# Layer 2 of a four-layer image network: from a scheduler's order to an order written out, with outer products moved to GpSimd

## The chip, the cores and the metric

The kernel runs on one core of one Trainium2 chip. A core has five engines that work side by side and wait for each other through semaphores: TensorE (PE in the profile, with its weight loads as PEld), VectorE (DVE), ScalarE (ACT), GpSimd (POOL) and SyncE (SP), which here only starts transfers. SBUF is the memory on the chip that they compute from, PSUM the one that TensorE writes to. The metric is the device time of one launch in microseconds. Before the change it is 10302.39 us, the median of three runs (10298.44 to 10305.17).

## What is computed

Four images of 256 channels and 64x64 pixels pass through four layers, each of the form `x = x + layer(group_norm(x))`: a deformable convolution (layer 0), an attention (layer 1), a deformable aggregation with 16 groups (layer 2) and a state-space scan (layer 3). The change touches layer 2 alone:

```
xp   = w_value . x + b_value                        # 256 channels = 16 groups x 16
om   = w_om . x + b_om                              # 432 = 16 groups x (9 points x (dx, dy) + 9 masks)
for each pixel (h, w), group g, point k of a 3x3 grid:
    sy, sx = h + ky[k] + dy[g,k],  w + kx[k] + dx[g,k]
    val    = bilinear sample of the zero-padded xp, group g, at (sy, sx)
    out[h, w, g, :] += mask[g,k] * val
y = w_out . out + b_out
```

Where no offset exceeds 1, every sample lies in a window of 5x5 pixels around its own. The kernel uses that: it works out, for each pixel and group, 25 shares (one for each place of the window) and sums 25 shifted copies of `xp` with them. If any offset does exceed 1, a last branch of the program computes everything anew in a slower way (`layer2_any`).

## The kernel before

The four images go one after the other; in each, layers 0 to 3 follow each other, and each needs the whole result of the one ahead. Layer 2 takes the image as 32 tiles. A tile is one row of the upper half of the image together with the row 32 below it, 2 x 64 = 128 pixels, one for each partition. The main loop (`for j0`) takes two tiles at a time (`T = 2`), so an image has 16 pairs.

For a pair the work is:

- `values(q)`: two rows of `xp` by matmuls (L701, L703), a copy into a ring of four tiles by ScalarE (L704), and eight transfers by SyncE (L708) that put the copies shifted by -2, -1, 1 and 2 pixels beside it. This is done for rows ahead of the pair.
- `shares(j0)`: offsets and masks by matmuls into a PSUM tile `pom` (L720, L723). ScalarE makes three weights of each offset, `relu(-o)`, `1 - |o|` and `relu(o)`, in `hat` (L727 to L730). VectorE takes the largest `|o|` for the test at the end (L732), multiplies one side's weights with the mask (L736, `mh`), forms the 3x3 outer products of the two sides (L744, `pr`, one instruction for each of two tiles), and adds them into the 5x5 shares `A` in PSUM, one instruction for each of 9 points and 2 tiles (L753). `A` has been cleared by ScalarE (L715). `shares` is a Python generator: the loop draws the next pair's steps between the products of the current pair.
- The five steps of the window (`for wy`): in each, VectorE multiplies five shifted copies with their shares, once for each of two tiles (L802, `prod`, three buffers); GpSimd adds the five products partly, four to two (L810); TensorE sums the remaining three into one PSUM tile `pd` by multiplying with the identity (L812).
- `finish`: ScalarE copies `pd` to SBUF (L820), TensorE transposes it (L762), ScalarE copies it back (L764), TensorE multiplies with `w_out` (L771), and VectorE adds the result to the image `x` (L780), with statistics for layer 3 at every fourth pair (L152). It is called during the next pair.

Within layer 2 the order of the code isn't the order on the engines: a scheduler places each engine's instructions, and the loop's order is its input. An engine runs its own instructions strictly in the order that they were placed in. `values`, `pt3` and `pz2` share one PSUM bank (`self.psum`), `pom` is one tile of two banks, and `A` has two tiles of two banks each.

Of the kernel before, what the change touches and what calls it, by code (L numbers as in the profile page):

```python
# [16 lines left out]
P = 128  # L17
# [46 lines left out]
class Net:  # L64
# [588 lines left out]
    def layer2(self, x):  # L653


        nc, tc = self.nc, self.tc
        gk, T = GRP * K2, 2
        with (
# [51 lines left out]
            def shares(j0):  # L710

                A = pshare.tile([P, T, 512], F32, tag="A", name="A")
                A = A[:, :, : GRP * WIN * WIN]
                made[j0] = A
                nc.scalar.copy(A, zero.rearrange("p (t u) -> p t u", u=1).to_broadcast([P, T, GRP * WIN * WIN]))  # L715
                A = A.rearrange("p t (g y x) -> p t g y x", y=WIN, x=WIN)
                po = pom.tile([P, T, 512], F32, tag="pom", name="pom")
                for t in range(T):
                    for ct in range(2):
                        nc.tensor.matmul(  # L720
                            po[:, t, : 3 * gk], xr[:, ct, j0 + t + 2, :], wom[:, ct, :], start=(ct == 0), stop=False
                        )
                    nc.tensor.matmul(po[:, t, : 3 * gk], self.halves[:, 0, :], bom, start=False, stop=True)  # L723

                hat = pb.tile([P, T, 2 * gk, 3], F32, tag="hat", name="hat")
                ab = pb.tile([P, T, 2 * gk], F32, tag="ab", name="ab")
                nc.scalar.activation(hat[:, :, :, 0], po[:, :, : 2 * gk], AF.Relu, scale=-1.0)  # L727
                nc.scalar.activation(hat[:, :, :, 2], po[:, :, : 2 * gk], AF.Relu)
                nc.scalar.activation(ab, po[:, :, : 2 * gk], AF.Abs)
                nc.scalar.activation(hat[:, :, :, 1], ab, AF.Identity, bias=1.0, scale=-1.0)  # L730
                yield
                nc.vector.tensor_reduce(  # L732
                    seen[:, j0 // T : j0 // T + 1], ab.rearrange("p t k -> p (t k)"), AX.X, ALU.max
                )
                mh = pb.tile([P, T, gk, 3], F32, tag="mh", name="mh")
                nc.vector.tensor_mul(  # L736
                    mh,
                    hat[:, :, 0:gk, :],
                    po[:, :, 2 * gk : 3 * gk].rearrange("p t (k u) -> p t k u", u=1).to_broadcast([P, T, gk, 3]),
                )  # L740
                yield
                pr = pb.tile([P, T, gk, 3, 3], F32, tag="pr", name="pr", bufs=1)
                for t in range(T):
                    nc.vector.tensor_mul(  # L744
                        pr[:, t],
                        mh[:, t].rearrange("p k (y x) -> p k y x", x=1).to_broadcast([P, gk, 3, 3]),
                        hat[:, t, gk : 2 * gk, :].rearrange("p k (y x) -> p k y x", y=1).to_broadcast([P, gk, 3, 3]),
                    )
                    yield
                for t in range(T):  # L750
                    for k in range(K2):
                        a = A[:, t, :, k // 3 : k // 3 + 3, k % 3 : k % 3 + 3]
                        nc.vector.tensor_add(a, a, pr[:, t, bass.ts(k, GRP), :, :])  # L753
                        if k % 3 == 2:
                            yield

            def finish(j0, o):
                oT = pb.tile([P, 2, 2, T, W], F32, tag="oT", name="oT")
                pt = self.ps("pt3")
                for ct in range(2):  # L760
                    for t in range(T):
                        nc.tensor.transpose(pt[:, bass.ts(2 * ct + t, P)], o[:, t, bass.ts(ct, P)], self.ident)  # L762
                for ct in range(2):
                    nc.scalar.copy(  # L764
                        oT[:, ct].rearrange("p h t x -> p t h x"),
                        pt[:, bass.ts(ct, T * P)].rearrange("p (t h x) -> p t h x", t=T, h=2),
                    )
                pz = self.ps("pz2").rearrange("p (o y) -> p o y", o=2)
                for ot in range(2):
                    for ct in range(2):  # L770
# [3 lines left out]
                            oT[:, ct].rearrange("p h t x -> p (h t x)"),  # L774
                            start=(ct == 0),
                            stop=(ct == 1),
                        )
                for ot in range(2):
                    xs = x[:, ot, :].rearrange("p (h y) -> p h y", h=2)[:, :, j0 * W : (j0 + T) * W]
                    nc.vector.scalar_tensor_tensor(  # L780
                        xs, pz[:, ot, :].rearrange("p (h y) -> p h y", h=2), bo[:, ot : ot + 1], xs, ALU.add, ALU.add
                    )
                    if j0 % 8 == 8 - T:
                        for h in range(2):
                            self.note(x, ot, 4 * h + j0 // 8)

            made, late = {}, None
            for q in range(3):
                values(q)
            for _ in shares(0):  # L790
                pass
            for j0 in range(0, HH, T):
                if j0 // VR + 3 < (HH + 4) // VR:
                    values(j0 // VR + 3)
                ahead = shares(j0 + T) if j0 + T < HH else iter(())
                A = made.pop(j0).rearrange("p t (g y x) -> p t g y x", y=WIN, x=WIN)
                pd = pacc.tile([P, T * 256], F32, tag="pacc", name="pacc")
                for wy in range(WIN):
                    prod = pb.tile([P, WIN, T, 256], F32, tag="prod", name="prod", bufs=3)
                    for t in range(T):  # L800
                        y = j0 + t + wy
                        nc.vector.tensor_mul(  # L802
                            prod[:, :, t, :].rearrange("p x (g c) -> p x g c", c=GC),
                            ring[y // VR % 4][:, :, y % VR, :].rearrange("p x (g c) -> p x g c", c=GC),
                            A[:, t, :, wy, :].rearrange("p g (x u) -> p x g u", u=1).to_broadcast([P, WIN, GRP, GC]),
                        )
                        next(ahead, None)
                    prod = prod.rearrange("p x t c -> p x (t c)")
                    for i in (0, 2):
                        nc.gpsimd.tensor_add(prod[:, i, :], prod[:, i, :], prod[:, i + 1, :])  # L810
                    for wx in (4, 0, 2):
                        nc.tensor.matmul(  # L812
                            pd, self.ident, prod[:, wx, :], start=(wy == 0 and wx == 4), stop=(wy == WIN - 1 and wx == 2)
                        )
                    if wy == 1 and late:
                        finish(*late)
                for _ in ahead:
                    pass
# [714 lines left out]
```

## Time and profile before

The profiled execution took 10256.01 us, and its span is 10254.2 us. In the first image layer 0 lies at about 0 to 620, layer 1 at 620 to 1138, layer 2 at 1138 to 1576 and layer 3 at 1576 to 2600.

| | PE | PEld | DVE | ACT | POOL | clock |
|---|---|---|---|---|---|---|
| whole span, share busy | 86% | 41% | 77% | 47% | 64% | 0.957 |
| layer 2, 1141.5 to 1575.9 (434.4 us), busy us | 387.41 | 165.89 | 408.59 | 94.61 | 242.24 | 0.98 |
| the same in image 2 (434.8 us) | 386.78 | 165.91 | 408.39 | 94.63 | 242.01 | 0.98 |
| image 3 (433.8 us) | 387.02 | 165.82 | 408.38 | 94.63 | 241.70 | 0.98 |
| image 4 (436.3 us) | 386.88 | 165.98 | 408.74 | 94.68 | 242.17 | 0.98 |

A row of the profile names the line of the kernel, the engine, the operation, the tile written and the tiles read (`prod<-ring,A`), the shape, and how often it ran. After the bar come busy time and the mean of one in ns, and after a second bar the time that the engine sat idle just before, with what ended that wait. "Clock" is the share of full speed that TensorE was granted. A timeline row has start and duration, and merges runs of like instructions (`x11`); an instruction's duration overlaps the next one's start, so what one costs in a row is read from start to start.

### The profile page before, as it was taken

Reading aid. Unit: us, or ns where it says so; the run is one execution under the profiler, and the core shown is the slowest. Engines: PE = TensorE matmul, PEld = TensorE weight load, DVE = VectorE, ACT = ScalarE, POOL = GpSimd, SP = SyncE. Lnnn points to the kernel's source line nnn. Section 1 sums busy time; section 2 is a strip of 40 time slices with the busy share of each in tenths; the row PEclk is TensorE's granted clock in tenths of the full one; section 3 lists DMA queues with packets and bytes.
Section 4 is the critical chain, followed back from the end, with each engine's and each line's share of the span. In section 5 each row is a group of like instructions: output and inputs, shape, how many; then the busy total and the mean of one; then the engine's idle time right before and its main releaser. Section 6 shows DMA issues by size and latency. Waiting matters only on the chain. (4 is left out here: it accounts for less than half of the span.)

```text
span 10254.2 us, 89063 instructions
## 1 busy us (share of the span) xinstructions
PE 8808.1 (86%) x29193; PEld 4231.4 (41%) x29193; DVE 7924.0 (77%) x8975; ACT 4869.3 (47%) x7460; POOL 6576.2 (64%) x3768
## 2 busy tenths in 40 slices
PE   5889998888788999889878898988977899888997
PEld 3643333333464333333346433333335643333333
DVE  4864697999675469799968546989996854798998
ACT  3743224665473322566557332256655733216664
POOL 3746556787474655688757465568875736556886
PEclk8999999999899999999989999999998999999999
DMA  7930111111782011111179101111118910111111
GB/s 264 328 109 1 37 40 35 44 45 49 269 315 97 1 37 40 36 45 46 45 286 325 70 1 41 36 40 48 44 43 321 322 36 1 45 41 37 40 41 34
DMA packets 377894, 956.57 MB, mean 93 GB/s; under 512 B 34676, under 2 KB 107821, under 8 KB 375373
## 3 DMA queue, kind: packets, MB, share of 16 engines
q0 software_dynamic: 165888, 604.05, 16.4%
q1 hardware_dynamic: 211532, 346.73, 10.6%
q8 instruction: 234, 3.83, 0.2%
q14 instruction: 240, 1.96, 0.1%
HBM read 784.59 MB, written 92.32 MB: 86 GB/s over the span
## 5 line engine op out<-in xcount | busy, mean ns | idle before, releaser
L1378 DVE TENSOR_TENSOR_SCAN h<-da,carry,h 128x512 f32<-128x512 f32 x2048 | 2470.6, 1264 | 140.2 <-ACT da L1377 91.4
L1392 POOL TENSOR_TENSOR h<-h,cn 128x2048 f32<-128x2048 f32 x508 | 2300.2, 4528 | 41.3 <-POOL carry L1389 0.6
L1377 ACT ACTIVATE da<-delta,l3a 128x512 f32<-128x512 f32 x2048 | 1388.7, 689 | 1145.5 <-DVE h L1378 1143.7
L1290 PE MATMUL y<-h,ident 128*128 128x512 f32 x4096 | 1920.9, 613 | 1.9 <-POOL h L1395 0.9
L344 POOL DMA_INDIRECT g<-tab,idx x1152 | 1343.7, 1166 | 761.0 <-issue 349.8
L548 POOL TENSOR_TENSOR acc<-acc,e 128x1024 f32<-128x1024 f32 x480 | 1125.3, 2344 | 541.0 <-ACT e L544 519.8
L810 POOL TENSOR_TENSOR prod<-prod 128x512 f32<-128x512 f32 x640 | 945.9, 1499 | 745.9 <-DVE prod L802 716.7
L388 PE MATMUL pz<-cols,l0w 128*128 128x256 f32 x4608 | 1213.6, 410 | 173.6 <-DVE cols L377 80.2
L1290 PEld LDWEIGHTS y<-h,ident 128*128 128x128 f32 x4096 | 806.0, 197 | 1289.3 <-issue 1236.8
L1370 DVE TENSOR_TENSOR h<-du,bn 128x2048 f32<-128x2048 f32 x512 | 1157.9, 2261 | 26.6 <-PE bn L1298 26.2
L465 DVE TENSOR_REDUCE m<-pm 128x3 f32<-128x1536 f32 (+1 forms) x372 | 602.3, 1625 | 716.8 <-PE pm L455 715.1
L353 DVE SCALAR_TENSOR_TENSOR r<-g,wx,r 128x512 f32<-128x512 f32 x1152 | 857.7, 745 | 352.3 <-ACT r L352 262.4
L812 PE MATMUL pacc<-prod,ident 128*128 128x512 f32 x1920 | 960.7, 623 | 142.7 <-POOL prod L810 106.2
L388 PEld LDWEIGHTS pz<-cols,l0w 128*128 128x128 f32 x4608 | 895.2, 205 | 341.5 <-DVE cols L377 117.7
L555 PE MATMUL cx<-e,v 128*128 128x512 f32 x2048 | 1001.4, 616 | 0.0
L544 ACT ACTIVATE e<-sc 128x1024 f32<-128x1024 f32 x512 | 496.0, 1020 | 1032.8 <-PE sc L531 1032.8
L802 DVE TENSOR_TENSOR prod<-ring,A 128x1280 f32<-128x1280 f32 x640 | 932.7, 1477 | 19.7 <-DMA ring<-ring 13.1
L352 ACT ACTIVATE r<-g,wx 128x512 f32<-128x512 f32 x1152 | 826.3, 717 | 254.8 <-DMA g<-tab,idx 209.2
L370 PE MATMUL pt<-ident,acc 128*128 128x128 f32 x2304 | 428.3, 293 | 302.0 <-DVE acc L361 197.5
L1389 POOL COPY carry<-h 128x4 f32<-128x4 f32 x512 | 98.3, 192 | 807.0 <-DVE h L1378 795.0
L812 PEld LDWEIGHTS pacc<-prod,ident 128*128 128x128 f32 x1920 | 325.9, 190 | 702.1 <-POOL prod L810 459.7
L555 PEld LDWEIGHTS cx<-e,v 128*128 128x128 f32 x2048 | 352.2, 189 | 598.9 <-issue 596.3
(247 smaller groups left out, 11219.4 us busy)
## 6 DMA issues: line engine op xcount, KB each, us to landing
cn<-cd SPq DMA_DIRECT2D x512, 256.0 KB
tab<-vt SPq DMA_DIRECT2D x112, 640.0 KB
ring<-ring SPq DMA_DIRECT2D x288, 126.0 KB
ring<-ring SPq DMA_DIRECT2D x288, 124.0 KB
g<-tab,idx POOLq DMA_INDIRECT x1152
x<-in_x SPq DMA_DIRECT2D x64, 256.0 KB
out<-x SPq DMA_DIRECT2D x56, 256.0 KB
l0w<-in_l0w SPq DMA_DIRECT2D x4, 2304.0 KB
```

Source lines behind the costliest of these rows:

```text
L344: nc.gpsimd.indirect_dma_start(out=g[:], out_offset=None, in_=tab[:, :], in_offset=bass.IndirectOffsetOnAxis(ap=idx[:, t, k : k + 1], axis=0),
L388: nc.tensor.matmul(sums[m][:, ot, :256], wf[:, i, bass.ts(ot, P)], cols[m][:, i, :], start=(i == 0), stop=(i == 17),)
L548: nc.gpsimd.tensor_add(b["acc"], b["acc"], e)
L555: nc.tensor.matmul(blocks[qb]["cx"], v[:, 4 * (i + kt // 4 * 4) + kt % 4, :], e[:, bass.ts(i % 2, 512)], start=(kt == 0 and i == 0), stop= ...
L802: nc.vector.tensor_mul(prod[:, :, t, :].rearrange("p x (g c) -> p x g c", c=GC), ring[y // VR % 4][:, :, y % VR, :].rearrange("p x (g c) - ...
L810: nc.gpsimd.tensor_add(prod[:, i, :], prod[:, i, :], prod[:, i + 1, :])
L812: nc.tensor.matmul(pd, self.ident, prod[:, wx, :], start=(wy == 0 and wx == 4), stop=(wy == WIN - 1 and wx == 2))
L1290: nc.tensor.matmul(c["ys"][dc], self.ident, h[:, dc, :], start=False, stop=(n == DS - 1))
L1370: nc.vector.tensor_mul(h, c["du"], c.pop(("bn", n)).to_broadcast([P, 4, C]))
L1377: nc.scalar.activation(da, c["delta"][:, dc, :], AF.Exp, scale=al[:, dc, n : n + 1])
L1378: nc.vector.tensor_tensor_scan(h[:, dc, :], da, h[:, dc, :], carry[:, dc, n : n + 1], ALU.mult, ALU.add)
L1392: nc.gpsimd.tensor_mul(h, h, cn.to_broadcast([P, 4, C]))
```

## The change

Layer 2's loop is written out for four engines (`tc.manual_schedule` for PE, Activation, DVE and Pool), so that each of them runs the instructions in the order of the code. SyncE's transfers are still placed by the scheduler. The generator is replaced by small functions, called from the five steps of each pair:

- `offsets(p + 2, t)` in steps 0 and 1, `hats(p + 2, ...)` in steps 2 and 3: a pair's offsets and weights are begun two pairs ahead. `values(p + 3)` stands in step 2.
- `masked(p + 1)` stands between the two products of step 0, `outer(p + 1, i)` in steps 0 to 2, `gather(p + 1, i)` in steps 2 to 4.
- `hat`, `mh` and `pr` hold the two tiles innermost by point, and `A` is one tile of 1024 elements in which groups and tiles lie together. One gather therefore serves both tiles: 9 instructions of 288 elements in place of 18 of 144.
- The outer products are three instructions of 864 elements on GpSimd. For the first pair two of the three stay on VectorE.
- `total`, the sum on TensorE, is called one step later than the additions whose results it reads. `turned` and `project` (parts of `finish`) come in steps 3 and 4 of the next pair, `finish` in step 1 of the one after.
- VectorE's maximum of `|o|` is replaced by a ScalarE instruction that sums `relu(|o| - 1)` as it goes, and the test at the end asks for more than 0 in place of more than 1.
- Ahead of the loop the first pair's offsets, hats and clearing come before the first `values`.

```diff
-                nc.vector.tensor_reduce(
-                    seen[:, j0 // T : j0 // T + 1], ab.rearrange("p t k -> p (t k)"), AX.X, ALU.max
-                )
...
-                for t in range(T):
-                    nc.vector.tensor_mul(
-                        pr[:, t],
-                        mh[:, t].rearrange("p k (y x) -> p k y x", x=1).to_broadcast([P, gk, 3, 3]),
-                        hat[:, t, gk : 2 * gk, :].rearrange("p k (y x) -> p k y x", y=1).to_broadcast([P, gk, 3, 3]),
-                    )
...
-                        nc.vector.tensor_add(a, a, pr[:, t, bass.ts(k, GRP), :, :])
...
+                    nc.scalar.activation(side(1), d["ab"], AF.Identity, bias=1.0, scale=-1.0)
+
+                    nc.scalar.activation(d["ab"], d["ab"], AF.Relu, bias=-1.0, accum_out=seen[:, p : p + 1])
...
+                engine.tensor_mul(
+                    d["pr"][:, bass.ts(i, n)],
+                    mh[:, bass.ts(i, n), :].rearrange("p k (y x) -> p k y x", x=1).to_broadcast([P, n, 3, 3]),
+                    hat[:, bass.ds(gk * T + i * n, n), :]
+                    .rearrange("p k (y x) -> p k y x", y=1)
+                    .to_broadcast([P, n, 3, 3]),
                 )
...
+                for k in range(3 * i, 3 * i + 3):
+                    a = A[:, :, i : i + 3, k % 3 : k % 3 + 3]
+                    nc.vector.tensor_add(a, a, made[p]["pr"][:, bass.ts(k, GRP * T)])
...
+                for t in range(T):
+                    offsets(0, t)
+                hats(0, 0)
+                hats(0, 1)
+                clear(0)
+                values(0)
+                masked(0)
+                for i in range(3):
+                    outer(0, i, nc.gpsimd if i == 1 else nc.vector)
+                values(1)
+                values(2)
+                for t in range(T):
+                    offsets(1, t)
+                for i in (0, 2, 1):
+                    gather(0, i)
+                hats(1, 0)
+                hats(1, 1)
+
+
+                behind = None
+                for p in range(last + 1):
+                    near, far = p < last, p < last - 1
+                    for wy in range(WIN):
+                        product(p, wy, 0)
+                        if near and wy == 0:
+                            masked(p + 1)
+                        product(p, wy, 1)
+                        if wy == 1 and p > 1:
+                            finish(p - 2)
+                        if near and wy > 1:
+                            gather(p + 1, wy - 2)
+                        if near and wy < 3:
+                            outer(p + 1, wy, nc.gpsimd)
+                        prod = pairs(p)
+                        if behind:
+                            total(*behind)
+                        behind = p, wy, prod
+                        if wy == 0:
+                            if near:
+                                clear(p + 1)
+                            if p:
+                                nc.scalar.copy(made[p - 1]["o"].rearrange("p t c -> p (t c)"), made[p - 1]["pd"])
+                        if far and wy < 2:
+                            offsets(p + 2, wy)
+                        if wy == 2:
+                            if far:
+                                hats(p + 2, 0)
+                            if p < last:
+                                values(p + 3)
+                        if wy == 3:
+                            if far:
+                                hats(p + 2, 1)
+                            if p:
+                                turned(p - 1)
+                        if wy == 4 and p:
+                            project(p - 1)
+                total(*behind)
...
-        nc.vector.tensor_scalar(i, m, 1.0, None, ALU.is_gt)
+        nc.vector.tensor_scalar(i, m, 0.0, None, ALU.is_gt)
```

## The prediction

> **What bounds the kernel now.** I first looked at which engine has no idle time in layer 2. A pair of tiles (a pass of the `j0` loop) takes 24.64 us: its first product starts at 1226.05 and the next pair's at 1250.69. The busy time of each engine in exactly that stretch (PE, PEld, DVE, ACT, POOL, then clock, DMA share, GB/s):
>
> ```profile
> 1226.05:1250.69 24.64, 22.95 (x62) 10.18 (x62) 24.20 (x34) 5.88 (x9) 14.93 (x10) 1.00 0.14 42
> ```
>
> VectorE is busy 24.20 of 24.64; TensorE looks almost as full, but its ends are modelled, so I go by starts. The groups of layer 2 from the list by shape say what the work is:
>
> ```profile
> L810 POOL TENSOR_TENSOR prod<-prod 128x512 f32<-128x512 f32 x640 | 945.9, 1499 | 745.9 <-DVE prod L802 716.7 <-PE pacc L812 28.3 <-DVE A L753 1.0
> L802 DVE TENSOR_TENSOR prod<-ring,A 128x1280 f32<-128x1280 f32 x640 | 932.7, 1477 | 19.7 <-DMA ring<-ring 13.1 <-DVE A L753 0.5
> ...
> L753 DVE TENSOR_TENSOR A<-A,pr 128x144 f32<-128x144 f32 x1152 | 358.2, 311 | 22.5
> ...
> L744 DVE TENSOR_TENSOR pr<-mh,hat 128x1296 f32<-128x1296 f32 x128 | 191.7, 1500 | 0.1
> ...
> L736 DVE TENSOR_TENSOR mh<-hat,pom 128x864 f32<-128x864 f32 x64 | 66.6, 1041 | 1.1 <-ACT hat L730 1.0
> ```
>
> L802 idles 19.7 us in 640 runs, and those mostly for ring copies: VectorE is the bound, and GpSimd waits for it (716.7). Durations overlap, so costs come from start to start in the timeline of VectorE (start, duration, count of the run):
>
> ```profile
> 1236.88 1.47 DVE L802 TENSOR_TENSOR prod<-ring,A 128x1280 f32<-128x1280 f32 x1
> 1238.28 0.30 DVE L753 TENSOR_TENSOR A<-A,pr 128x144 f32<-128x144 f32 x1
> 1238.49 1.47 DVE L802 TENSOR_TENSOR prod<-ring,A 128x1280 f32<-128x1280 f32 x1
> ...
> 1245.82 1.04 DVE L736 TENSOR_TENSOR mh<-hat,pom 128x864 f32<-128x864 f32 x1
> 1246.78 3.81 DVE L753 TENSOR_TENSOR A<-A,pr 128x144 f32<-128x144 f32 x11
> 1250.69 4.28 DVE L802 TENSOR_TENSOR prod<-ring,A 128x1280 f32<-128x1280 f32 x3
> ```
>
> A product costs 1.40; a gather between products 0.21; eleven in a row take 3.91, so one behind its forerunner costs 0.37 (it reads what that wrote). L736 costs 0.96; from the same timeline L744 1.41, L732 0.66, the two L780 0.785. Sum: 10 x 1.40 + 7 x 0.21 + 3.91 + 2 x 1.41 + 0.66 + 0.96 + 0.785 = 24.6, the period. Every fourth pair adds four statistics, 2.38.
>
> **VectorE after.** The outer products leave (2.82) and so does the maximum (0.66). The 18 gathers of 144 elements become 9 of 288. Elements cost (1.41 - 0.96) / (1296 - 864) = 1.04 ns, so 144 more cost 0.15: one alone 0.36, one behind its forerunner 0.52; three in a row 1.40, and three such groups 4.2 (before 5.4). No row shows the new layout of A (groups and tiles together), so I bound a group by 1.2 (forerunners cost nothing extra: 3 x 0.36, rounded up) and 2.0 (each as dear again as its elements), and take 1.40. New sum: 14.0 + 4.2 + 0.96 + 0.785 = 19.95, and with a quarter of 2.38, 20.5.
>
> **TensorE after.** Nothing is removed, only put in order. Start to start:
>
> ```profile
> 1228.26 1.72 PE L720 MATMUL pom<-l,xr 128*128 128x432 f32 x4
> 1229.91 0.35 PE L723 MATMUL pom<-bom,halvesb 3*128 3x432 bf16 x1
> 1230.19 1.98 PE L812 MATMUL pacc<-prod,ident 128*128 128x512 f32 x4
> ...
> 1237.94 1.03 PE L701 MATMUL pc<-l,xr 128*128 128x256 f32 x4
> ...
> 1240.38 8.25 PE L812 MATMUL pacc<-prod,ident 128*128 128x512 f32 x18
> ```
>
> Offsets of a tile: 1.93, twice 3.86. Values: 1240.38 - 1237.94 = 2.44. An L812 costs 0.43 (weight loads start 0.43 apart), 30 make 12.9. Four transposes 0.49, the projection 1.93. Sum 21.62. This exceeds VectorE's 20.5, so TensorE becomes the bound. The totals lie one step behind the products and offsets two pairs ahead, so TensorE should rarely wait; a hand-over from GpSimd costs 0.05 (end 1232.89, start 1232.94), and five a pair make 0.25. The granted clock is 1.00 here and where TensorE is fuller (720 to 1120, layer 1), so density costs no clock.
>
> **GpSimd after, and two rules.** It keeps ten additions and gets three products of 864 elements; no row shows a GpSimd operand with rows of three elements and a repeated one.
>
> ```profile
> 1229.08 3.81 POOL L810 TENSOR_TENSOR prod<-prod 128x512 f32<-128x512 f32 x2 [6.28 <-DVE prod L802]
> 1233.29 3.63 POOL L810 TENSOR_TENSOR prod<-prod 128x512 f32<-128x512 f32 x2 [0.40 <-DVE prod L802]
> 1238.50 2.50 POOL L810 TENSOR_TENSOR prod<-prod 128x512 f32<-128x512 f32 x2 [1.58 <-DVE prod L802]
> ```
>
> Two additions take 2.50 except beside L744, where they take 3.81 and 3.63. L548 does 1024 elements in 2.344 and L810 512 in 1.271 (its median), so an element costs (2.344 - 1.271) / 512 = 2.1 ns and an instruction 0.2 besides; 864 take 0.2 + 864 x 2.1 ns = 2.0. Sum 5 x 2.50 + 3 x 2.0 = 18.5, below 21.62. The lower end is 1.9 (a repeated element costing nothing to read again); for the upper end I double the element's price for the short rows, 0.2 + 864 x 4.2 ns = 3.8. I take 2.0, the end by plain rows, which are the nearest.
>
> The Trainium skill speaks against the move: "GPSIMD Engine Reference", section "When to use GPSIMD", sends elementwise work to VectorE, GpSimd being about twice as slow with two inputs. The rows agree on the price (6.0 against 2.82 a pair). By the rule alone, adding 6.0 - 2.82 = 3.2 to a pair, 24.64 becomes 27.8 and the kernel loses 64 x 3.2 = 205 us; by the rows the 6.0 falls into GpSimd's idle time (9.7 of 24.64), and the rule does not bind. A second rule decides how deep that idle time is: "SBUF — State Buffer", section "SBUF: two separate sides", says that a VectorE instruction with two SBUF inputs and a GpSimd one that reads SBUF lock each other out for a whole instruction. L744 is VectorE's only such instruction in the loop (products, gathers and L736 read PSUM too), and it goes. By the rule additions take 2.50 everywhere: 18.5. If instead the mean of 1499 stayed, 15.0 + 6.0 = 21.0. Either fits below 21.62.
>
> **ScalarE after.** Four hats stay, written at twice the stride, and a sum of 576 elements comes (0.65 to 1.0, between L729 and L730). 5.9 busy becomes about 6.7. Were the hats twice as long, 9.5 of 21.6 would still be covered: they are due three steps after their offsets.
>
> **Start, end and queues.** The first image's stage runs from the first L186 (1141.5) to the end of the last L780 (1575.9), 434.4 us. At its start the ring copies bind: the eighth product waited for the third ring tile until 1190.8.
>
> ```profile
> 1187.61 0.30 DVE L753 TENSOR_TENSOR A<-A,pr 128x144 f32<-128x144 f32 x1
> 1190.82 1.49 DVE L802 TENSOR_TENSOR prod<-ring,A 128x1280 f32<-128x1280 f32 x1 [2.90 <-DMA ring<-ring]
> ```
>
> SyncE's queue holds only these copies here, 24 issues from 1149.34, behind the first L704. In the new order that copy stands behind pair 0's offsets on TensorE (about 6.5 at the start's granted clock of 0.50, where an L720 takes 0.72, done near 1149.9), its hats and the clearing of A on ScalarE (5.2): the first issue moves to about 1156, 6.6 later, and so the eighth product, to 1197.4. Then come 1.4 + 1.4 (gather) + 2.8 + 1.4, and pair 1 starts at 1204.4; before it was 1201.41. Loss 3.0. In the loop a ring tile is made about 22 us before use and lands 15 to 16 after issue (one pair's copies move from 1241 to 1257): covered. At the end the totals are a step behind, six L812 or 2.58, part of it beside other work: loss about 2.0.
>
> **Sum for an image.** Pairs 1 to 14 took 350.7 (1201.41 to 1552.13). After: two pairs at VectorE's 19.95 until three product tiles are full, 11 at 21.62 + 0.25, pair 14 (no offsets) at 20.0: 300.5. Gain 50.2 - 3.0 - 2.0 = 45.2; four images 181. The profiled execution took 10256.0 with a span of 10254.2; it would become 10075. The median, 10302.4, lies 46 above it; the same gain makes 10121.
>
> **Rivals.** Pairs 1 to 14 took 350.7 / 14 = 25.05 on average, statistics included, and 5 of an image's gain go at its ends. (a) Gathers at 2.0 a group: VectorE's 19.95 + 1.8 + 0.6 = 22.35 binds; gain 14 x 2.7 - 5 = 33 an image, 10171. For it: the new stride in A; against: L753 and the larger rows fit one price an element. Chance 0.08. (b) GpSimd binds: three products of 3.2 to 3.8, pair 22.1 to 23.9, gain 36 to 11, 10157 to 10258, taken at 10200. For and against as in the next. Chance 0.06. (c) Slower: the outer products on GpSimd past a point. With the ends' 5 the pairs must stay under 25.05 - 0.36 = 24.7; 12.5 + 3 x O exceeds that from O = 4.06, twice the plain row. At O = 5 a pair takes 27.5, an image 14 x 2.45 + 5 = 39 more: 10459. For it: no row shows such operands; against: with full rows 512, 1024 and 2048 elements all follow 2.1 ns. Chance 0.08. (d) A wait takes the gain's place: TensorE's fixed order holds totals behind offsets, which wait for `masked`, behind hats. For it: offsets already waited for L736 once at the start (1171.08); against: `masked` stands between the first two products, steps ahead of need. The waits would have to eat 45 an image, to within 0.2% of the time (20 us), about what a measurement of this kernel can tell from no change. Chance 0.03. The forecast has 0.75.
>
> **Range and chances.** Without the losses at both ends and with the pairs at 21.62 exactly the gain is 53 an image; the start could give 4 more, since three ring tiles are sent ahead of pair 0 and not four: 57, or 10075. Upwards the range takes in (a) and (b): 10205; beyond lie (c), (d). Left out are (c) and (d), half of (b) and 0.05 of the forecast below. Faster 0.75 + 0.08 + 0.06 = 0.89, same 0.03, slower 0.08.
>
> **What would show it.** Pairs about 21.8 apart; VectorE waiting for the totals, TensorE without gaps; three GpSimd products of about 2.0 a pair and additions at 1.27 throughout; gathers 0.36 and 0.52 apart; the first ring copy later by 6 to 7. A GpSimd product over 3.2 makes the forecast wrong; over 4.06, its sign too.

## The result and the profile after

The changed kernel takes 10140.26 us, the median (10133.2 to 10144.41), beside 10300.42 us for the kernel before (10279.46 to 10305.17). The ratio is 0.9847, with a 95% interval from 0.9832 to 0.9863. The forecast was 10121.

To see where the 160 us come from I measure the stage that the prediction used, from the first L186 of layer 2 to the end of the last addition to `x` (L780 before, L811 after), in the profiled execution of each kernel:

| layer-2 stage, us | image 1 | 2 | 3 | 4 | sum | image 1: to the start of pair 1 | pairs 1 to 14 | pair 15 to the end |
|---|---|---|---|---|---|---|---|---|
| before | 434.4 | 434.8 | 433.8 | 436.3 | 1739.3 | 59.9 | 350.7 | 23.7 |
| after | 391.6 | 392.5 | 392.0 | 392.3 | 1568.4 | 64.0 | 300.2 | 27.4 |

The stages lose 170.9 us, 42.7 an image. The rest of the program, which the change does not touch, took 8514.9 in the profile of before (10254.2 - 1739.3) and 8574.2 in that of after (10142.6 - 1568.4). That difference has the other sign, and most of it belongs to the one execution: the profile of before was 46 us quicker than its median. Taken from the medians, the rest is 8561.1 (10300.42 - 1739.3) and 8571.9 (10140.26 - 1568.4), which are 10.8 apart. So I compare stages, not spans, below.

First the busy times of the engines in pair 7, exactly from its first product to the next pair's (PE, PEld, DVE, ACT, POOL, then clock, DMA share, GB/s):

```profile
1354.73:1376.18 21.45, 21.45 (x64) 10.69 (x63) 19.91 (x22) 7.25 (x11) 17.76 (x14) 1.00 0.16 48
```

A pair takes 21.45 where it took 24.64. TensorE is now busy throughout; VectorE has 1.5 us to spare and GpSimd 3.7. The list by shape, over the whole run, has the rows of layer 2:

```profile
L823 DVE TENSOR_TENSOR prod<-ring,A 128x1280 f32<-128x1280 f32 x640 | 922.4, 1480 | 122.7 <-DMA ring<-ring 102.7 <-PE pacc L840 15.3 <-issue 0.9
L840 PE MATMUL pacc<-prod,ident 128*128 128x512 f32 x1920 | 915.3, 610 | 37.7 <-DVE prod L823 23.7 <-POOL prod L832 8.8 <-ACT o L900 2.7
...
L832 POOL TENSOR_TENSOR prod<-prod 128x512 f32<-128x512 f32 x640 | 800.3, 1274 | 187.8 <-DVE prod L823 170.1 <-PE pacc L840 17.1 <-DVE A L779 0.5
...
L766 POOL TENSOR_TENSOR pr<-mh,hat 128x864 f32<-128x864 f32 x184 | 332.6, 1808 | 207.8 <-DVE mh L746 207.8
...
L779 DVE TENSOR_TENSOR A<-A,pr 128x288 f32<-128x288 f32 x576 | 267.0, 464 | 13.5
...
L736 ACT ACTIVATE hat<-pom 128x576 f32<-128x576 f32 x64 | 81.4, 1271 | 0.0
```

GpSimd's wait for products fell from 716.7 to 170.1, and its additions from a mean of 1499 ns to 1274. VectorE now waits, for ring copies most of all (102.7, before 13.1); by its timeline 82.8 of these lie in the first pairs of the four images, and 17.8 in pairs 1 to 14. In the same list, limited to 1271.4 to 1512.3, the middle of the first image, TensorE's sums wait for nothing:

```profile
L840 PE MATMUL pacc<-prod,ident 128*128 128x512 f32 x338 | 158.0, 603 | 0.0
```

VectorE's timeline of the same pair shows the gathers in threes (1.46 long; from 1364.88 to 1366.56 less the wait of 0.22 is 1.46, and 1370.17 to 1371.53, where nothing waits, 1.36) and the small waits for TensorE and for ring copies, with which its spare time is filled:

```profile
1364.88 1.46 DVE L779 TENSOR_TENSOR A<-A,pr 128x288 f32<-128x288 f32 x3
1366.56 1.49 DVE L823 TENSOR_TENSOR prod<-ring,A 128x1280 f32<-128x1280 f32 x1 [0.22 <-PE pacc L840]
1368.76 1.49 DVE L823 TENSOR_TENSOR prod<-ring,A 128x1280 f32<-128x1280 f32 x1 [0.72 <-DMA ring<-ring]
1370.17 1.46 DVE L779 TENSOR_TENSOR A<-A,pr 128x288 f32<-128x288 f32 x3
1371.53 2.87 DVE L823 TENSOR_TENSOR prod<-ring,A 128x1280 f32<-128x1280 f32 x2
```

The start of the stage (L186 at 1165.8) went as follows; the first line is SyncE's queue, the others VectorE:

```profile
1181.48 30.00 SPq L709 DMA_DIRECT2D ring<-ring  x24
...
1222.69 1.49 DVE L823 TENSOR_TENSOR prod<-ring,A 128x1280 f32<-128x1280 f32 x1 [5.23 <-DMA ring<-ring]
...
1229.82 1.49 DVE L823 TENSOR_TENSOR prod<-ring,A 128x1280 f32<-128x1280 f32 x1
```

The first ring copy is issued 15.7 after the L186, before the change 7.8; the eighth product comes 56.9 after it, before 49.3; pair 1 starts 64.0 after it.

VectorE's timeline shows one wait that the prediction does not have. `L922`, the reduction of the test sums, stands behind the loop in the code. The scheduler put it in the middle of pair 13, where it waits for ScalarE's last sum:

```profile
1504.66 0.17 DVE L922 TENSOR_REDUCE m<-seen 128x1 f32<-128x16 f32 x1 [3.65 <-ACT ab L741]
```

The next gaps in TensorE's timeline, the first since 1271.4, begin at 1512.3, 8 us later:

```profile
1513.97 1.10 PE L840 MATMUL pacc<-prod,ident 128*128 128x512 f32 x2 [1.66 <-DVE prod L823]
1515.66 3.21 PE L840 MATMUL pacc<-prod,ident 128*128 128x512 f32 x6 [0.59 <-POOL prod L832]
1519.86 2.35 PE L840 MATMUL pacc<-prod,ident 128*128 128x512 f32 x4 [0.99 <-POOL prod L832]
```

### The profile page after: what moved, and what is told of

Same layout as the page of the kernel before. It is cut to its first block, busy times and chain, and to the rows that moved or that the text cites. A ratio compares the mean times of both kernels' runs of the same rounds, so it can differ in the third digit from the quotient of the medians.

```text
span 10142.6 us, 88824 instructions
## 1 busy us (share of the span) xinstructions
PE 8738.3 (86%) x29189; PEld 4281.7 (42%) x29193; DVE 7651.8 (75%) x8215; ACT 4961.6 (49%) x7588; POOL 6768.8 (67%) x3952
## 3 DMA queue, kind: packets, MB, share of 16 engines
q1 hardware_dynamic: 211532, 346.73, 10.8%
## 4 chain that ended last, share of the span: by engine, by line
PE 24%; DVE 9%; ACT 5%; issue 4%; POOL 4%; DMA 3%; another core or an unknown queue 1%; SPq 0%; POOLq 0%; DVEq 0%; ACTq 0%
PE cx L555 5%; DVE h L1476 4%; PE pacc L840 3%; PE y L1388 2%; DMA g<-tab,idx 2%; PE pm L455 2%; PE front L1236 2%; POOL h L1490 2%; DVE h L1468 2%; PE sc L531 2%; PE front L1190 1%; ACT da L1475 1%; DVE r L353 1%; POOL g L344 1%; DMA ring<-ring 1%
## 5 line engine op out<-in xcount | busy, mean ns | idle before, releaser
L1490 POOL TENSOR_TENSOR h<-h,cn 128x2048 f32<-128x2048 f32 x508 | 2300.0, 4527 | 41.1 <-POOL carry L1487 0.4
L823 DVE TENSOR_TENSOR prod<-ring,A 128x1280 f32<-128x1280 f32 x640 | 922.4, 1480 | 122.7 <-DMA ring<-ring 102.7
L840 PE MATMUL pacc<-prod,ident 128*128 128x512 f32 x1920 | 915.3, 610 | 37.7 <-DVE prod L823 23.7
L832 POOL TENSOR_TENSOR prod<-prod 128x512 f32<-128x512 f32 x640 | 800.3, 1274 | 187.8 <-DVE prod L823 170.1
L360 ACT ACTIVATE acc<-r,wy 128x256 f32<-128x256 f32 x1152 | 571.4, 496 | 28.0 <-DVE r L353 22.4
```

The costliest lines, as they stand in the source:

```text
L823: nc.vector.tensor_mul(d["prod"][:, :, t, :].rearrange("p x (g c) -> p x g c", c=GC), ring[y // VR % 4][:, :, y % VR, :].rearrange("p x (g ...
L840: nc.tensor.matmul(d["pd"], self.ident, prod[:, wx, :], start=(wy == 0 and wx == 4), stop=(wy == WIN - 1 and wx == 2),)
L1490: nc.gpsimd.tensor_mul(h, h, cn.to_broadcast([P, 4, C]))
```

## The experiments

The theory is the prediction's: VectorE bound the loop, the change takes work from it until TensorE's sum of 21.6 a pair binds, and GpSimd's products fit in its idle time. Three questions follow: which part of the change does it, whether TensorE is the limit, and where the losses at the start, the end and in between lie. All results, each ratio against the kernel before on the same chip, and the stages (us) from the profile:

| kernel | ratio [95%] | stages, sum | image 1: start | pairs 1 to 14 | end |
|---|---|---|---|---|---|
| before | | 1739.3 | 59.9 | 350.7 | 23.7 |
| changed | 0.9847 [0.9832, 0.9863] | 1568.4 | 64.0 | 300.2 | 27.4 |
| outer products alone | 0.9847 [0.9831, 0.9864] | 1589.8 | 62.8 | 311.0 | 23.7 |
| all but the outer products | 0.9974 [0.9965, 0.9984] | 1716.4 | 66.2 | 336.5 | 26.8 |
| no fixed order | 0.9867 [0.985, 0.9883] | 1598.6 | 63.9 | 311.5 | 23.9 |
| maximum on VectorE | 0.9817 [0.9801, 0.9833] | 1563.6 | 63.4 | 299.8 | 26.8 |
| a fifth of the sums short | 0.9814 [0.9797, 0.983] | 1541.2 | 65.8 | 291.5 | 28.5 |
| outer products twice | 0.9946 [0.9931, 0.9961] | 1684.0 | 64.0 | 326.5 | 29.7 |
| values first | 0.9814 [0.98, 0.9828] | 1538.7 | 57.2 | 300.2 | 27.3 |
| no lag of the sums | 0.9882 [0.9864, 0.99] | 1616.4 | 64.8 | 306.4 | 33.8 |
| test sums reduced last | 0.9835 [0.9822, 0.9849] | 1555.1 | 65.0 | 297.0 | 27.5 |
| values first, more additions | 0.9771 [0.9756, 0.9786] | 1500.1 | 56.7 | 289.6 | 28.6 |
| the same with an earlier end | 0.9782 [0.9766, 0.9798] | 1505.3 | 56.7 | 288.8 | 30.8 |
| changed, on another chip | 0.9841 [0.9825, 0.9856] | 1571.7 | 64.5 | 300.2 | 27.8 |

### Which part brings the gain

**Outer products alone.** The kernel before with one word changed:

```diff
-                    nc.vector.tensor_mul(
+                    nc.gpsimd.tensor_mul(
                         pr[:, t],
```

> The kernel before with one part of the change alone: its two outer products a pair are issued on GpSimd. VectorE's pair falls from 24.64 to 21.8, GpSimd's work becomes 12.5 + 2 x 2.6 = 17.7. Theory (the order is needed as well): waits take back much of it, a pair of 23 to 24, 10210 to 10260. Rival (relief of VectorE alone): a pair of 21.8 to 22.2, 10140 to 10165.

The ratio is the whole change's, and the stages fall by 149.5 of the 170.9 us. The rival is right. A pair of this kernel, by windows (the columns as above):

```profile
1237.00:1258.80 21.80, 21.79 (x63) 10.49 (x62) 21.36 (x33) 5.83 (x9) 17.54 (x13) 1.00 0.15 48
```

and two rows of its list by shape over the whole run:

```profile
L810 POOL TENSOR_TENSOR prod<-prod 128x512 f32<-128x512 f32 x640 | 797.3, 1277 | 140.6 <-DVE prod L802 123.9 <-DVE A L753 8.7 <-PE pacc L812 7.9
...
L744 POOL TENSOR_TENSOR pr<-mh,hat 128x1296 f32<-128x1296 f32 x128 | 329.0, 2592 | 279.8 <-DVE A L753 159.2 <-DVE mh L736 74.7 <-ACT oT L764 42.6
```

The prediction's rows say why: 24.64 less two L744 (2.82) is 21.82, and 21.80 is measured. With that VectorE stands a third of a microsecond above TensorE's 21.45, so what else it gives up can hardly count. What is left for the rest of the change are those 0.35 a pair and the statistics, which still cost 2.4 in three pairs of an image here (24.17) and are absorbed in the changed kernel. Together pairs 1 to 14 fall by a further 10.8; start and end give 4.9 of it back.

**All but the outer products.** The changed kernel with the products of the loop left on VectorE:

```diff
                         if near and wy < 3:
-                            outer(p + 1, wy, nc.gpsimd)
+                            outer(p + 1, wy, nc.vector)
```

> The changed kernel with the loop's outer products back on VectorE, order kept. Theory: VectorE's sum becomes 14.0 + 4.2 + 0.96 + 0.785 + 3 x 0.96 = 22.8, with statistics 23.4, and it binds again; the additions beside the outer products take longer than 1.27 again; 14 x 4 x 1.9 = 106 more than the changed kernel, 10245. Rival (moving them is worth nothing, TensorE binds either way): 10125 to 10155.

Only 22.9 of the 170.9 us are left, less than expected. A pair takes 23.50. From the prediction's terms, 24.64 less 1.2 for gathers and 0.66 for the maximum, 22.78 was due. Two of a pair's three L766 in VectorE's timeline, and GpSimd's additions beside them:

```profile
1342.55 1.05 DVE L766 TENSOR_TENSOR pr<-mh,hat 128x864 f32<-128x864 f32 x1
1343.52 2.88 DVE L823 TENSOR_TENSOR prod<-ring,A 128x1280 f32<-128x1280 f32 x2
...
1347.10 1.62 DVE L766 TENSOR_TENSOR pr<-mh,hat 128x864 f32<-128x864 f32 x1
1348.64 1.47 DVE L823 TENSOR_TENSOR prod<-ring,A 128x1280 f32<-128x1280 f32 x1
```

```profile
1342.77 3.18 POOL L832 TENSOR_TENSOR prod<-prod 128x512 f32<-128x512 f32 x2 [2.84 <-DVE prod L823]
1346.54 3.33 POOL L832 TENSOR_TENSOR prod<-prod 128x512 f32<-128x512 f32 x2 [0.59 <-DVE prod L823]
```

The L766 at 1342.55 begins ahead of an addition and costs 0.97, and the additions take 3.18 in place of 2.50; the one at 1347.10 begins while an addition runs, and costs 1.54 to the next product. That is 0.57 of the missing 0.72; the other 0.15 stays open. Two engines hold each other up here, and putting the products on GpSimd ends that for both.

**No fixed order.** The changed kernel, with its order left to the scheduler:

```diff
-            with tc.manual_schedule(
...
-            ):
+            with ExitStack():
```

> The changed kernel with the fixed order taken away: the same functions called in the same sequence, but the scheduler places the instructions of all engines. Theory (the fixed order is what keeps TensorE fed, and TensorE's own 21.6 us of work a pair is the bound): the scheduler again puts work ahead of the totals and TensorE waits for GpSimd, a pair takes 22.5 or more, 10190 or more. Rival (the gain is VectorE's relief alone, in whatever order): a pair stays at 21.5 to 21.8, 10125 to 10155.

It came out between the two: the stages are 30.2 longer than with the fixed order. Pairs 1 to 14 average 22.25 and not 21.44. A row of its list by shape, 1260 to 1500, shows where:

```profile
L811 DVE SCALAR_TENSOR_TENSOR x<-pz,l,x 128x256 f32<-128x256 f32 x22 | 10.5, 477 | 25.3 <-PE pz L799 25.3
```

In eleven pairs VectorE waits 25.3 us for the projection; in the written order the addition comes in step 1 of the pair after the projection, and doesn't wait. Left to the scheduler, the changed code is 8.8 us behind the outer products alone (1598.6 to 1589.8, one profile of each, on one chip), so the other parts gain nothing there: they pay only in the written order.

**Maximum on VectorE.** ScalarE's sum is taken out and VectorE's maximum put back, in the fixed order:

```diff
-                    nc.scalar.activation(d["ab"], d["ab"], AF.Relu, bias=-1.0, accum_out=seen[:, p : p + 1])
...
             def masked(p):
                 d = made[p]
+                nc.vector.tensor_reduce(seen[:, p : p + 1], d["ab"].rearrange("p t k -> p (t k)"), AX.X, ALU.max)
```

(and the test at the end asks for more than 1 again.)

> The changed kernel with the largest offset taken by VectorE again (0.66 us a pair, just ahead of the mask product) and no sum on ScalarE; order kept. Theory (TensorE binds, VectorE has 21.5 - 20.5 = 1.0 to spare): a pair stays at 21.5, at most 10 us more than the changed kernel, a ratio to before of 0.984 to 0.986. Rival (what leaves VectorE counts in full): 14 x 4 x 0.66 = 37 more, 0.988.

Moving the maximum was worth nothing: the stages are 4.8 shorter without it. VectorE's plain pair becomes 20.69, and with statistics 23.32, 21.35 on average: still under TensorE's 21.45. What the move to ScalarE does cost is L922's wait, which this kernel doesn't have. It has a smaller loss of its own. `L923`, which follows L922 and takes the larger of two numbers in each partition, begins just after an outer product on GpSimd and ends with it: it takes 1.79, in the changed kernel 0.15, and pair 14 takes 22.26. VectorE's row, then GpSimd's:

```profile
1505.62 1.79 DVE L923 TENSOR_TENSOR omax<-omax,m 128x1 f32<-128x1 f32 x1
```

```profile
1505.61 1.78 POOL L766 TENSOR_TENSOR pr<-mh,hat 128x864 f32<-128x864 f32 x1
```

### Whether TensorE is the limit

**A fifth of the sums short.** TensorE adds two of the three partial sums; the fifth product is left out of the result:

```diff
-                for wx in (4, 0, 2):
+                for wx in (0, 2):
...
```

> The changed kernel without the sums of the fifth product of each step: they are left out, so layer 2 loses that part of its result and TensorE loses 10 x 0.43 = 4.3 us a pair. Theory (TensorE is the bound, VectorE the next at 20.5): a pair falls by about 1.1 and no more, VectorE's idle time in the loop goes to nothing, 10075 to 10095. Rival (the three product tiles and the hand-overs between three engines set the pair, not TensorE's work): at most 0.3 a pair, 10120 to 10140.

The theory holds in kind. The list by shape, 1260 to 1500:

```profile
L823 DVE TENSOR_TENSOR prod<-ring,A 128x1280 f32<-128x1280 f32 x114 | 163.9, 1479 | 1.2
...
L840 PE MATMUL pacc<-prod,ident 128*128 128x512 f32 x227 | 122.7, 637 | 27.1 <-POOL prod L832 22.8
```

Now TensorE waits and VectorE does not: the pair is 20.02, VectorE's sum as predicted (19.95). The stages gain 27.2, less than I had expected, because the statistics are on the path again (22.65 in every fourth pair) and start and end (65.8 and 28.5) gain nothing.

**Outer products twice.** Each product in the loop is issued twice on GpSimd; the second repeats the first's result:

```diff
...
-                            outer(p + 1, wy, nc.gpsimd)
+                            for _ in range(2):
+                                outer(p + 1, wy, nc.gpsimd)
```

> The changed kernel with each of the loop's outer products issued twice on GpSimd (same result, 3 x 1.8 = 5.4 us more GpSimd work a pair). GpSimd's work was 17.9 of 21.5 us. Theory (3.6 us of GpSimd's time a pair were idle, and only what exceeds TensorE's 21.5 counts): GpSimd's sum becomes 12.5 + 10.8 = 23.3, a pair goes from 21.5 to about 23.4, 14 x 4 x 1.9 = 106 more than the changed kernel, a ratio to the kernel before near 0.995. Rival (GpSimd's work was on the path already): 14 x 4 x 5.4 = 300 more, 1.014.

GpSimd binds, in rows of its list by shape (1260 to 1500) that hardly wait:

```profile
L832 POOL TENSOR_TENSOR prod<-prod 128x512 f32<-128x512 f32 x106 | 131.8, 1274 | 0.0
L766 POOL TENSOR_TENSOR pr<-mh,hat 128x864 f32<-128x864 f32 x61 | 109.0, 1788 | 2.4
```

The pair is 23.14, and 5 x 2.50 + 6 x 1.79 = 23.2. With a product's price doubled to 3.58 the stages still gain 13.8 an image. A microsecond more a product costs 14 x 3 = 42 an image, so the gain would be gone at about 3.58 + 13.8 / 42 = 3.9; the prediction put that point at 4.06.

### Where the losses lie

**Values first.** The start with the rows of `xp` ahead of most of the first pair's offsets:

```diff
+                values(0)
+                values(1)
                 for t in range(T):
                     offsets(0, t)
+                values(2)
                 hats(0, 0)
                 hats(0, 1)
                 clear(0)
-                values(0)
...
-                values(1)
-                values(2)
```

> The changed kernel with the start of each image in another order: values of the first two ring tiles ahead of the first pair's offsets on TensorE, the third behind them, and the ring copies ahead of the hats on ScalarE. Theory (ring copies bind the start; in the changed kernel the first is issued 7.9 us later than before): the first copy is issued about 7 earlier, pair 1 starts 4 to 7 earlier, 16 to 28 us less than the changed kernel, a ratio to before of 0.982 to 0.983. Rival (the start is set by VectorE's shares of the first pair, which now come later): no gain, 0.9845 to 0.986.

The stages fall by 29.7, 7.4 an image, all at the start. L186 is at 1157.4 here; the timelines of ScalarE and VectorE:

```profile
1165.25 0.58 ACT L705 COPY ring<-pc 128x512 f32<-128x512 f32 x1 [6.34 <-PE pc L704]
```

```profile
1207.50 1.49 DVE L823 TENSOR_TENSOR prod<-ring,A 128x1280 f32<-128x1280 f32 x1 [2.53 <-DMA ring<-ring]
```

The first ring tile is copied 7.8 after the L186 (in the changed kernel 15.1), and the eighth product comes at 50.1 in place of 56.9: ring copies set the start, as the prediction read from the profile of before.

**No lag of the sums.** `total` follows its own step's additions directly; the copy of the last pair's sums is moved ahead of it:

```diff
-                        if behind:
-                            total(*behind)
-                        behind = p, wy, prod
+                        if wy == 0 and p:
+                            nc.scalar.copy(made[p - 1]["o"].rearrange("p t c -> p (t c)"), made[p - 1]["pd"])
+                        total(p, wy, prod)
...
```

> The changed kernel with each step's totals called right behind its additions, not one step later (offsets and values of a step then stand behind its totals on TensorE). Theory (TensorE, once loaded, is behind the products by itself, so the written lag decides little; at the end of an image it costs): pairs stay at 21.5, the end is 2 to 3 us shorter an image, 0 to 12 less than the changed kernel. Rival (the lag is what keeps TensorE from waiting for GpSimd): TensorE waits up to 2.5 us in steps, a pair of 23 or more, 80 or more above the changed kernel.

It cost 44.7 against the same kernel on that chip (1616.4 to 1571.7), which neither side had expected. In the first image 6.2 of it lie in pairs 1 to 14 and 6.0 behind them. The 6.2 are a balance: the reduction of the test sums now stands in pair 14, where it waits 0.45, so that pair 13 takes 23.14 in place of 26.27. Against these 3.1 stand some 9 us of losses, of two kinds. TensorE's timeline has the first kind in most pairs, at the sums of step 0:

```profile
1329.14 3.46 PE L840 MATMUL pacc<-prod,ident 128*128 128x512 f32 x6
```

Six sums take 2.74 without a wait; here 0.72 more, for GpSimd's additions. In the ten pairs from 1241 on these waits come to 4.5 us. The second kind is in VectorE's timeline, in pair 2, which takes 24.70 for 20.03, and in the last pair:

```profile
1207.57 1.49 DVE L823 TENSOR_TENSOR prod<-ring,A 128x1280 f32<-128x1280 f32 x1 [2.90 <-DMA ring<-ring]
...
1492.83 4.28 DVE L823 TENSOR_TENSOR prod<-ring,A 128x1280 f32<-128x1280 f32 x3 [4.57 <-DMA ring<-ring]
...
1504.22 0.88 DVE L811 SCALAR_TENSOR_TENSOR x<-pz,l,x 128x256 f32<-128x256 f32 x2 [7.11 <-PE pz L799]
```

In this order `values` stands behind the sums of its own step, so ring tiles are made later; that this is why pair 2 and the last pair wait for ring copies is my reading, which no run separates from the rest.

**Test sums reduced last.** The test sums of all images stay in one tile and are reduced once, in the code behind the last layer:

```diff
...
-            nc.vector.tensor_reduce(m1, seen, AX.X, ALU.max)
-            nc.vector.tensor_max(self.omax, self.omax, m1)
...
     def far(self):
...
+        nc.vector.tensor_reduce(self.omax, self.seen, AX.X, ALU.max)
```

> The changed kernel, with the images' test sums kept in one tile and reduced once behind the last layer, so that the reduction of the sums (L922) no longer stands in VectorE's order in the middle of pair 13 of every image, where it idled 3.65 us for ScalarE's last sum (15.2 us in four images). Theory: VectorE was the later engine there, since TensorE, without a gap until then, waited 1.66 + 0.59 + 0.99 us for products and additions directly behind it; so the wait was on the path, and pairs 13 and 14 together take about 43 us in place of 46.3; the layer-2 stage falls by 3.0 to 3.7 us an image, 12 to 15 in all (1553 to 1557 us against 1568.4), ratio near 0.983. Rival: TensorE's backlog covers the wait (its order was full until 1512.3, and the products' buffers would hold VectorE anyway), and the stage falls by less than 1 us an image, within 4 us of 1568.4 in all.

The theory holds in three of the four images. In the first, pairs 13 and 14 take 22.66 + 20.03 where they took 26.34 + 20.03, and pairs 1 to 14 of the first three fall by 3.2, 3.9 and 3.9. In the fourth, the scheduler has put the one reduction that is left (L927 here) into pair 13 again:

```profile
8792.60 0.22 DVE L927 TENSOR_REDUCE omax<-seen 128x1 f32<-128x64 f32 x1 [3.84 <-ACT ab L743]
```

There pair 13 takes 26.59, and pairs 1 to 14 take 300.2 as in the changed kernel. So the wait costs 11.0 us in three images, 3.7 in each. All four stages fall by 13.3 (1568.4 to 1555.1), the rest of it at starts and ends, where one chip differed from another by 3.3 in this sum. The total alone could not have told it: 0.9835 and 0.9847 have overlapping intervals.

### A better version, and one that wasn't

**Values first, more additions.** As TensorE binds and GpSimd has 3.7 us a pair, GpSimd takes a third addition in steps 3 and 4, where it has no outer product, and TensorE two L840 less in each of these steps:

```diff
...
                     nc.gpsimd.tensor_add(prod[:, i, :], prod[:, i, :], prod[:, i + 1, :])
+                if wy > 2:
+                    nc.gpsimd.tensor_add(prod[:, 2, :], prod[:, 2, :], prod[:, 4, :])
...
-                for wx in (4, 0, 2):
+                for wx in (0, 2) if wy > 2 else (4, 0, 2):
```

(with the start of the kernel "values first".)

> The changed kernel with the other start order as above, and in steps 3 and 4 of each pair a third addition on GpSimd, so that TensorE sums two products there in place of three: TensorE loses 2 x 0.86 = 1.7 us a pair (19.8), GpSimd gains 2.5 (20.4), VectorE stays at 20.5 with statistics. Theory (the largest of the three sums binds): a pair of 20.6 on average, 14 x 4 x 0.8 = 45 less than with the other start alone, a ratio to before near 0.978. Rival (with three engines near 20.4 the three product tiles cannot even out the steps): no gain over the other start alone, 0.982 or more.

At 0.9771 it is the fastest of all, 38.6 shorter in the stages than "values first". VectorE binds again, at 20.03 a pair (22.66 with statistics), which its list by shape (1260 to 1500) shows by the short waits of VectorE's products:

```profile
L823 DVE TENSOR_TENSOR prod<-ring,A 128x1280 f32<-128x1280 f32 x116 | 167.0, 1480 | 1.4 <-issue 0.2
```

**The same with an earlier end.** In the last pair the sums follow at once, pair 14's `finish` comes in the last step, and the statistics follow both additions to `x`:

```diff
...
                         behind = p, wy, prod
+                        if p == last and wy:
+                            total(*behind)
+                            behind = None
...
                             project(p - 1)
+                            if p == last:
+                                finish(p - 1)
...
```

> The kernel with the other start and the third addition (0.9771 of the kernel before), with the last pair's totals called at once, the last but one finished in its last step, and the statistics behind both additions to the image. Theory (the last pair has room on TensorE, and a lag only delays its end): 2 to 4 us less an image, 8 to 16 less, a ratio to before of 0.9755 to 0.9765. Rival (the end hangs on the chain of the last sum, two copies and two multiplications, not on the lag): no change, 0.9770.

Nothing came of it: the stages are 5.2 longer, of which the other chip makes some 3.3 (1571.7 to 1568.4 for the changed kernel), and the ratios cannot be told apart. The end itself takes 30.8 in place of 28.6, although two statistics that lay inside it now lie behind it. The rival, that the end hangs on the chain from the last product through sums, transposes and projection, fits; how much of the 27.4 could be saved otherwise stays open.

**The changed kernel on another chip**, the one on which the kernels without the lag and with an earlier end were run:

> The changed kernel itself, beside the two below on one chip, so that they can be compared with it directly. 0.9847 of the kernel before is expected.

The medians are 9919.6 and, before, 10083.9. The stage sum, 1571.7, and the ratio, 0.9841, agree with 1568.4 and 0.9847.

## Why the prediction was right, step by step

The number was right, 10121 for 10140.26, and so was the mechanism: the work leaves VectorE, TensorE's sum becomes the bound, and GpSimd's share fits below it. Step by step:

- **VectorE 19.95.** 20.02 where VectorE binds (the kernel with fewer sums, and pair 2 of the changed one). A group of three gathers costs 1.36 to 1.46, as the 1.40 had it. Right, and rival (a) falls with it.
- **TensorE 21.62 and 0.25 for hand-overs.** 21.45, and no hand-over costs anything, since TensorE has no gap. That was 0.42 too much in each of 11 pairs, 4.6 an image.
- **Statistics.** Absorbed in pairs 5 and 9: a pair with them takes 22.66, the one behind it 20.24, together two of 21.45. Pair 13 has no such pair behind it, since pair 14 has no offsets to make: in the run with the test sums reduced last the two take 22.66 and 20.03, and the statistics cost 1.2.
- **What the prediction did not see: L922.** The diff leaves the reduction behind the loop, and I read it there. Before the change the scheduler had put it into pair 14, where it waited for nothing; now it stands in pair 13 and waits for ScalarE; the run with the test sums reduced last puts 3.7 us an image on that. Pairs 1 to 14 of the first image came out at 300.2 for a predicted 300.5 because this wait and the hand-overs that do not exist nearly cancel; without L922's wait they take 297.0 (296.3 in the second and third image). That agreement was luck.
- **GpSimd 2.0 a product.** 1.79 to 1.81, below even the lower end of 1.9. Since (1.79 - 0.2) / 864 = 1.84 ns an element and (2.59 - 0.2) / 1296 = 1.84 in the other shape, the assumption that failed is that a repeated operand costs at least as much as a plain one. That these are multiplications and not additions is no way out: layer 3's multiplication in full rows (L1490, 2048 elements in 4.53) costs 2.1 an element like the additions. Rivals (b) and (c) needed 3.2 and 4.06; the run with doubled products shows that their arithmetic was sound, and only their price did not occur.
- **The two rules.** "By the rule alone" the move was to cost 205 us; that move alone gained 149.5, because it fell into idle time and took VectorE off the path. By the second rule the lock was to go with L744, and it did: additions take 1274 ns with the products gone from VectorE, 1466 on average with them back.
- **ScalarE.** The hats take 1.22 to 1.27 for 0.96 to 0.99, and ScalarE is busy 7.25 of a pair and not 6.7. Covered, as argued; but the sum on ScalarE, counted as a relief of 0.66 for VectorE, brought nothing.
- **Start 3.0.** 4.1: the first ring copy was issued 7.9 later, not 6.6, and the eighth product came 7.6 later. The prediction moved the ring tiles back together; in fact the third is copied 10.9 us behind the first (L705 at 1180.87 and 1191.77), before the change 8.4 (L704 at 1148.73 and 1157.08). The granted clock has part in that: four L702 took 2.07 at 1181.51, where the clock was 0.50, and 1.13 at 1175.26, where it was 1.00. **End 2.0.** 3.7, of which 1.3 are two statistics that now stand between the two additions to `x`. Mechanisms right, sizes short by 2.8 an image together.
- **The sum.** 45.2 an image predicted, 42.7 measured: 171 us in the stages for 181. The medians differ by 160; at an interval of 0.0016 of the time on either side, 16 us, that is not distinguishable from 171.
- **Rival (d)**, a wait in the gain's place, came true only in small: the one of L922.

What the prediction never asked is which part does it. Its own rows had the answer: taking the two L744 away leaves 21.82 beside TensorE's 21.62, so nearly nine tenths of the gain (149.5 of 170.9) were in one word of the code, and everything else worked on the last few tenths of a microsecond.

## What to carry to other kernels

When a bound is taken away in several parts, subtract them one by one and stop at the next engine's sum: what comes after is worth little, and here one engine name gave 149.5 of 170.9 us. Idle time of a slow engine is worth using for work that the busy engine does faster, if the slow engine's whole sum stays below the next bound; afterwards look for that bound again, as one more addition on GpSimd gave another 38.6. When an order is written out, price its start and end apart from its loop, and look where the scheduler puts the instructions just behind it.

## What the runs showed of the hardware

- A product on GpSimd whose operands repeat each element three times, in rows of three, costs 1.84 ns an element beside 0.2 us an instruction, less than the 2.1 ns of its plain additions and multiplications.
- A VectorE instruction with two SBUF operands that begins during a GpSimd product lasts until about the end of that product and its own time more, and the reverse holds too. In the first pair of the changed kernel VectorE's L766 runs from 1180.53 to 1181.58; GpSimd's, begun at 1180.58, ends at 1183.22 and takes 2.65 for 1.79; VectorE's next, begun at 1181.50, takes 2.63 for 1.05. Even an instruction of one element a partition took 1.79 in place of 0.15, to the end of the product beside it (L923, with the maximum on VectorE).
- ScalarE writes 576 elements in 1.22 to 1.27 us at twice the stride of before (0.96 to 0.99), and in 0.65 to 0.70 where they lie together.
- The other chip ran everything outside layer 2 of the changed kernel in 8338.7 us where the first took 8574.2, at a mean granted clock of 0.959 and 0.950, with the layer-2 stages alike within 0.3%. No run here says why.
